# Sort loop of a graph network: the last one-hot tile in buffers of its own, and all gather products ahead of the counting

## The chip, the core and the metric

The kernel runs on one core of a Trainium2 chip. A core has five engines that run side by side, each with its own queue of instructions, and that wait for each other through semaphores: TensorE (matrix products; in the profile PE for the products and PEld for the loads of the stationary operand), VectorE (DVE), ScalarE (ACT), GpSimd (POOL) and SyncE (SP, which here only starts transfers). TensorE writes into PSUM, a small memory from which VectorE and ScalarE read; all other tiles lie in SBUF. The metric is the device time of one execution in microseconds, the median of several runs; lower is better.

## What is computed

The reference is a stack of four graph layers on 12,500 nodes with 412,500 directed edges, each between a layer norm with ReLU. The first layer is the one that matters here:

```python
h = jnp.maximum(_layernorm(x, axis=-1), 0.0)
x_j = h[dst]
m = jnp.einsum('ei,ej,ijh->eh', x_j, edge_attr_8, W_msg_tp) * norm
m = silu(m) @ W_msg_lin * norm_lin
agg = segment_sum(m, src)          # messages summed at the source nodes
```

For each edge the features of its destination node meet eight edge attributes and a weight table, pass through SiLU, and are summed at its source node. Three more layers (L1, L2 with layer norms on 64-wide edge features, L3) use the same edges again.

## The kernel before

**The sort.** The edges come ordered by destination. Before the layers, one loop (`sort_edges`, L355) brings them into a fixed layout that all layers then use. The nodes are cut into 98 windows of 128 destination nodes. Inside a window, edges are sorted into 128 cells by their source's block (`S`), 32 places a cell: that makes `TC` = 32 tiles of 128 edges. Edges beyond 32 in a cell go to `TO` = 5 more tiles, "the tiles beyond the cells". So a window has `TT` = 37 tiles. The loop runs twice over 49 windows (L400), and each pass is written out instruction by instruction with a fixed order on TensorE, VectorE, ScalarE and SyncE: these engines' order is that of the Python code, and no scheduler changes it.

**A step.** In step `g` of a pass several windows are at work, each at another age. The newest (age 0) has its records loaded: `keys` computes each edge's cell, `hot_cells` (L511) makes a one-hot tile of it, and `count` (L513 to L521) multiplies that with a triangle and with ones on TensorE, 36 products in bf16 into the PSUM bank `po`, so that each edge learns how many come before it. The window of age 1 has `look_up`, `rank` and `scatter` (L523 to L594): VectorE reads the counts out of `po` (L528 is the first instruction), works out the row of each edge, and GpSimd writes the records there with 35 indirect transfers (L588). `look_up` of a window stands at the head of the step after its count. Two and one steps before the oldest age the sorted records are read back, their slots transposed (`slot_rows`, L604) and loaded (`load_rows`).

**The first layer's messages, for the oldest window** (age 5, `old`). They are made in the same step. `hot_rows` (L615), one step ahead, turns slots into one-hot tiles on VectorE: three tiles, one for each of `PARTS`, 16, 16 and 5 edge tiles wide. `gather(i)` (L623) multiplies four of the 37 edge tiles at a time with the window's node table `win`, in f32 on TensorE, into a PSUM bank `pl`, of which there are two: gathers 0 to 3 read the first one-hot tile, 4 to 7 the second, and 8 and 9 (four tiles and one) the third. `products(i)` (L633) multiplies bank `i` with the edge attributes on VectorE and so frees the bank. `message(p)` (L648) sums and applies SiLU. `hot_sources` (L643) makes a further one-hot tile on VectorE, and `to_sources` (L661 to L666) uses it in 32 f32 products that add the messages at their sources.

**The order around the change.** In the second half of a step the code reads (L434 to L454): products 4, gather 6, products 5, gather 7; `count` of the new window; `hot_sources`, products 6, gather 8, products 7, gather 9, message 1; `hot_rows` of the next window; products 8 and 9, message 2, `to_sources`. On TensorE the count thus stands between gather 7 and gather 8. All three one-hot tiles of `hot_rows` come from one group of three buffers, so each is written where the same tile of the step before lay.

Of the kernel before, what the change touches and what calls it, by code (L numbers as in the profile page):

```python
# [11 lines left out]
F32 = mybir.dt.float32  # L12
# [7 lines left out]
P = 128  # L20
# [10 lines left out]
TC = CELLS * CAP // P  # L31
TO = 5
# [17 lines left out]
def tile_gnn(ctx: ExitStack, tc: tile.TileContext, a: dict, out: bass.AP):  # L50
# [15 lines left out]
    @contextmanager  # L66
    def banks(**bufs):

        with tc.tile_pool(name="psum", bufs=1, space=bass.MemoryType.PSUM) as pool:
            now[:] = [(pool, bufs)]  # L70
            yield
# [252 lines left out]
    def window_starts(wk):  # L324


        n = NB * TS
        di = wk.tile([P, n], I32, name="ws_di")
        sp.dma_start(di, a["dst"].rearrange("(p j) -> p j", p=P))
        v.tensor_single_scalar(di, di, 7, op=ALU.arith_shift_right)  # L330
        df = wk.tile([P, n], F32, name="ws_df")
        v.tensor_copy(df, di)
        est = wk.tile([P, P], F32, name="ws_est")
        part = wk.tile([P, P], F32, name="ws_part")
        hit = wk.tile([P, n], F32, name="ws_hit")
        at = wk.tile([P, 4], F32, name="ws_at")
        num = wk.tile([P, 4], F32, name="ws_num")
        v.memset(est, 0.0)
        for j in range(4):
            v.tensor_scalar(at[:, j:j + 1], df[:, 0:1], float(j), None, op0=ALU.add)  # L340
            v.tensor_scalar(hit, df, at[:, j:j + 1], None, op0=ALU.is_equal)
            v.tensor_reduce(num[:, j:j + 1], hit, AX.X, ALU.add)
            v.tensor_scalar(part, iota_row, at[:, j:j + 1], num[:, j:j + 1], op0=ALU.is_gt, op1=ALU.mult)
            v.tensor_add(est, est, part)
        every = wk.tile([P, P], F32, name="ws_every")
        gp.partition_all_reduce(every, est, P, bass_isa.ReduceOp.add)
        v.tensor_copy(est_i, every[0:1, :])
# [7 lines left out]
    def sort_edges():  # L355


        with tc.tile_pool(name="ws", bufs=1) as wk:
            window_starts(wk)
        with tc.tile_pool(name="so1", bufs=1) as one, tc.tile_pool(name="so", bufs=2) as ed, \  # L360
                banks(acc=4, po=1, pc=1, pl=2):
            k = {}
            k["empty"] = one.tile([P, TT, WORDS], F32, name="empty")
            v.memset(k["empty"], 0.0)
            v.memset(k["empty"][:, :, W_LS:W_LD + 1], NONE)
            k["tri"] = one.tile([P, P], BF16, name="tri")
            gp.memset(k["tri"], 1.0)
            gp.affine_select(out=k["tri"], in_=k["tri"], compare_op=ALU.is_gt, fill=0.0, base=0,
                             pattern=[[1, P]], channel_multiplier=-1)
            k["ones_bf"] = one.tile([P, P], BF16, name="ones_bf")  # L370
            v.memset(k["ones_bf"], 1.0)
            k["ones_f"] = one.tile([P, P], F32, name="ones_f")
            v.memset(k["ones_f"], 1.0)
            k["before"] = one.tile([P, TL, TL], F32, name="before")
            gp.memset(k["before"], 1.0)
            gp.affine_select(out=k["before"], in_=k["before"], compare_op=ALU.is_gt, fill=0.0, base=0,
                             pattern=[[1, TL], [-1, TL]], channel_multiplier=0)
            k["dump"] = one.tile([P, TL], F32, name="dump")
            gp.iota(k["dump"], pattern=[[P, TL]], base=ND * RM, channel_multiplier=1,
                    allow_small_or_imprecise_dtypes=True)  # L380
            v.memset(tall, 0.0)
            v.memset(cur, 0.0)

            nought = one.tile([P, 512], BF16, name="nought")
            v.memset(nought, 0.0)
            acc = [bank("acc") for _ in range(4)]
            for b in acc:
                pe.matmul(b, lhsT=nought[:, 0:P], rhs=nought, start=True, stop=True, skip_group_check=True)

            k["cells"] = dram_disjoint_views(cells, SG)  # L390
            k["slots"] = dram_disjoint_views(slot_lo, SG)

            k["parted"] = [one.tile([P, TC, 4, 16], F32, name=f"parted{b}") for b in range(2)]
            for t in k["parted"]:
                v.memset(t, 0.0)
            k["ps"] = bank("po")
            k["pc"] = bank("pc")
            v.tensor_copy(k["pc"][:, 0:P], iota_row)
            et = mybir.EngineType
            with tc.For_i(0, ND, SG) as i, tc.manual_schedule(engines={et.PE, et.DVE, et.Activation, et.SP}):  # L400
                ws = [Window(i, g, k, ed) for g in range(SG)]
                ws[0].load()
                for g in range(SG + LAG):
                    def at(lag):
                        return [ws[g - lag]] if 0 <= g - lag < SG else []
                    for w in at(-1):
                        w.load()
                    for w in at(LAG - 2):
                        w.read_back()
                    for w in at(LAG - 1):  # L410
                        w.load_rows()
                    for w in at(1):
                        w.look_up()
                        w.rank()
                        w.scatter()
                    old, new = at(LAG), at(0)
                    for w in old:
                        w.gather(0)
                        w.gather(1)
                        w.products(0)  # L420
                        w.gather(2)
                        w.products(1)
                        w.gather(3)
                    for w in new:
                        w.keys()
                    for w in old:
                        w.products(2)
                        w.gather(4)
                        w.products(3)
                        w.gather(5)  # L430
                        w.message(0)
                    for w in new:
                        w.hot_cells()
                    for w in old:  # L434
                        w.products(4)
                        w.gather(6)
                        w.products(5)
                        w.gather(7)
                    for w in new:
                        w.count()  # L440
                    for w in old:
                        w.hot_sources()
                        w.products(6)
                        w.gather(8)
                        w.products(7)
                        w.gather(9)
                        w.message(1)
                    for w in at(LAG - 1):
                        w.hot_rows()
                    for w in old:  # L450
                        w.products(8)
                        w.products(9)
                        w.message(2)
                        w.to_sources(acc)  # L454
                    for w in at(LAG - 2):
                        w.slot_rows()
                v.tensor_scalar(cur, cur, float(SG * P), None, op0=ALU.add)
            ok = one.tile([1, 1], F32, name="ok")
            v.tensor_scalar(ok, tall[0:1, 0:1], float(E), None, op0=ALU.is_equal)
            v.scalar_tensor_tensor(cells_i, tall[0:1, 1:2], float(TO * P), ok, op0=ALU.is_le, op1=ALU.mult)  # L460
            got = ed.tile([C, CELLS, 16], F32, name="wide", bufs=1)
            by_bank = got.rearrange("n (q b t) f -> b n t q f", q=4, b=4)
            for b in range(4):
                for q in range(4):
                    sc.copy(by_bank[b][:, :, q, :], acc[b][0:C, :].rearrange("n (t q f) -> n t q f", t=8, q=4)[:, :, q, :])
            with tc.If(nc.values_load(cells_i[0:1, 0:1], min_val=0, max_val=1) > 0):
                sp.dma_start(t_acc.rearrange("(s q) f -> q s f", q=C), got)

    class Window:
# [145 lines left out]
        def hot_rows(self):  # L615

            self.hots, self.got = [], {}
            for t0, k in PARTS:
                hot = self.ed.tile([P, 16 * P], F32, name="hot_dt0", bufs=3)
                v.tensor_scalar(hot[:, :k * P], self.u[:, t0 * P:(t0 + k) * P], iota_col, None, op0=ALU.is_equal)  # L620
                self.hots.append(hot)

# [1037 lines left out]
```

## Time and profile before

| | us |
|---|---|
| median of three runs | 21783.42 (21761.8 to 21790.21) |
| profiled execution | 22519.72 |
| its span, first to last instruction | 22518.0 |
| sort loop, first pass without its start and end | 470 to 3564 |
| sort loop, second pass without its start and end | 3991 to 7059 |
| mean granted TensorE clock | 0.75 |

| engine | busy us | share of the span |
|---|---|---|
| PE (products) | 15015.6 | 67% |
| PEld (loads) | 12155.3 | 54% |
| DVE | 13682.8 | 61% |
| POOL | 6955.3 | 31% |
| ACT | 3671.3 | 16% |

A row of the profile names the line of the kernel, the engine, the operation, the tiles (out<-in), the shapes and a count; after the first bar stand the busy time in all and the mean of one in ns, after the second the idle time of the engine just before such instructions and what ended most of it. "<-remote" there means that a semaphore came and that no instruction of the core was on record just before it. In a time line the columns are start, duration, engine, line, operation, and in brackets the idle time before it. Ends of TensorE's products are modelled, not seen. The profiled execution is 736 us longer than the median run without the profiler.

### The profile page before, as it was taken

How to read it: one execution, taken by the hardware profiler on the slowest of the kernel's cores; microseconds unless marked ns; L12 is line 12 of the kernel's file. 1: busy time of each engine (PE TensorE's matmuls, PEld its weight loads, DVE VectorE, ACT ScalarE, POOL GpSimd, SP SyncE). 2: the span in 40 equal slices, each digit the busy share in tenths (PEclk: the TensorE clock that was granted, in tenths of full speed). 3: DMA queues.
4: the chain of work that ended last, by engine and by line, in shares of the span. 5: the costliest groups of instructions: out<-in, count | busy, mean ns of one | idle time of the engine just before them, and what ended most of it. 6: DMA issues, size and time to landing. Idle time of an engine off the chain costs nothing. (4 is left out here: it accounts for less than half of the span.)

```text
span 22518.0 us, 475030 instructions
## 1 busy us (share of the span) xinstructions
PE 15015.6 (67%) x201276; PEld 12155.3 (54%) x201641; DVE 13682.8 (61%) x23150; ACT 3671.3 (16%) x8161; POOL 6955.3 (31%) x6387
## 2 busy tenths in 40 slices
PE   2444443444445888876666788888798988666665
PEld 1444443344444666655656566666566666544544
DVE  4666666666665666745555466666476765455455
ACT  0000000000001555510000122222222222000000
POOL 3444444444553333311111011111022221233233
PEclk7666666666666999967777699899799997566566
DMA  1000010000001222211111243344333332121121
GB/s 60 26 26 28 27 30 24 28 28 28 28 28 27 71 68 68 71 29 31 31 31 31 75 128 121 119 125 125 101 108 102 107 96 76 43 51 50 43 51 51
DMA packets 1081319, 1344.35 MB, mean 60 GB/s; under 512 B 474914, under 2 KB 629010, under 8 KB 1078374
## 3 DMA queue, kind: packets, MB, share of 16 engines
q1 hardware_dynamic: 799088, 1232.52, 17.4%
q0 software_dynamic: 258720, 76.68, 3.4%
q8 instruction: 1638, 26.84, 0.5%
q10 hardware_dynamic: 21462, 4.95, 0.1%
q14 instruction: 411, 3.37, 0.0%
HBM read 954.24 MB, written 359.21 MB: 58 GB/s over the span
## 5 line engine op out<-in xcount | busy, mean ns | idle before, releaser
L588 POOL DMA_INDIRECT cells<-rec,s_row x3430 | 3418.3, 997 | 3488.0 <-DVE s_row L584 2237.1
L630 PE MATMUL pl<-win,hot_dt 128*128 128x128 f32 x7252 | 1461.5, 371 | 2038.2 <-DVE wide L639 1533.3
L1350 POOL DMA_INDIRECT xo<-t_src,c x980 | 1139.8, 1163 | 5279.7 <-ACT lod L1095 1912.4
L630 PEld LDWEIGHTS pl<-win,hot_dt 128*128 128x128 f32 x7252 | 1341.0, 278 | 2143.9 <-DVE wide L639 1569.3
L1005 PE MATMUL po<-tab,hot_s 98*32 98x16 f32 x75264 | 1458.2, 204 | 1215.2 <-issue 725.5
L997 DVE TENSOR_TENSOR hot_d<-iota_row,c 128x1024 f32<-128x1024 f32 (+1 forms) x1470 | 1649.4, 1141 | 867.0 <-PE pa L1046 499.7
L664 PE MATMUL acc<-parted,hot_s 128*98 128x64 f32 x6272 | 1219.2, 352 | 1296.8 <-issue 1287.5
L1005 PEld LDWEIGHTS po<-tab,hot_s 98*32 98x32 f32 x75264 | 1240.8, 138 | 1473.6 <-issue 1154.2
L1119 DVE TENSOR_REDUCE nsum<-sq 128x8 f32<-128x512 f32 (+1 forms) x1470 | 946.6, 644 | 1588.9 <-ACT sq L1116 1422.9
L1010 POOL DMA_INDIRECT xw<-t_gc,c x980 | 1102.8, 1125 | 2545.3 <-DMA c<-cells 980.9
L664 PEld LDWEIGHTS acc<-parted,hot_s 128*98 128x98 f32 x6272 | 1117.9, 269 | 1419.3 <-issue 1409.8
L1164 PE MATMUL pa<-hot,y 128*64 128x128 f32 x21756 | 1686.0, 286 | 174.7 <-issue 92.7
L1133 DVE TENSOR_TENSOR hot<-iota_row,lod 128x512 f32<-128x512 f32 x2352 | 1513.7, 685 | 1.5 <-remote 1.1
L1046 PE MATMUL pa<-prod,hot_d 128*128 128x130 f32 x7252 | 1227.5, 336 | 416.4 <-DVE prod L1040 373.5
L1164 PEld LDWEIGHTS pa<-hot,y 128*64 128x64 f32 x21756 | 1244.0, 140 | 452.9 <-issue 192.9
L620 DVE TENSOR_SCALAR hot_dt<-u,iota_col 128x2048 f32<-128x2048 uint8 (+1 forms) x294 | 296.2, 1038 | 1961.2 <-remote 1883.2
L1116 ACT ACTIVATE sq<-po 128x512 f32<-128x512 f32 (+1 forms) x1470 | 831.0, 565 | 3668.4 <-PE po L1113 2995.0
L1046 PEld LDWEIGHTS pa<-prod,hot_d 128*128 128x128 f32 x7252 | 1129.1, 243 | 456.7 <-issue 434.8
L770 POOL DMA_INDIRECT g_l<-summed,row x490 | 810.2, 1653 | 1675.3 <-ACT summed L766 1447.7
L1386 PE MATMUL po<-ft,eb_w0e 128*64 128x512 f32 (+1 forms) x3920 | 1030.5, 594 | 296.8 <-DMA ft<-e_feat 276.9
L1010 POOL DMA_INDIRECT xo<-t_h,c x490 | 478.5, 976 | 2317.4 <-DMA c<-cells 1249.4
L1453 PE MATMUL pa<-hot_d,xw 128*32 128x128 f32 x14504 | 897.7, 374 | 369.3 <-DVE xw L1445 164.6
(363 smaller groups left out, 27049.8 us busy)
## 6 DMA issues: line engine op xcount, KB each, us to landing
e_feat<-ft SPq DMA_DIRECT2D x882, 256.0 KB
ft<-e_feat SPq DMA_DIRECT2D x882, 256.0 KB
c<-cells SPq DMA_DIRECT2D x392, 296.0 KB
places<-slot_lo SPq DMA_DIRECT2D x294, 392.0 KB
ud<-slot_lo SPq DMA_DIRECT2D x98, 1024.0 KB
c<-cells SPq DMA_DIRECT2D x147, 592.0 KB
us<-slot_lo SPq DMA_DIRECT2D x98, 784.0 KB
u<-slot_lo SPq DMA_DIRECT2D x98, 592.0 KB
```

What stands on the lines that cost most here:

```text
L588: ins = gp.indirect_dma_start(out=self.cells, out_offset=bass.IndirectOffsetOnAxis(ap=self.row[:, t:t + 1], axis=0), in_=self.rec[:, t, :] ...
L630: pe.matmul(pl[:, t * P:(t + 1) * P], lhsT=self.hots[t0 // 16][:, o:o + P], rhs=self.win, start=True, stop=True, skip_group_check=True)
L664: pe.matmul(acc[t // 8][0:C, o:o + 64], lhsT=self.hot[:, t, :], rhs=self.k["parted"][self.g % 2][:, t, :, :].rearrange("p q f -> p (q f)") ...
L997: v.tensor_tensor(o[:, :k, :], bc_mid(iota_row, k), bc_last(c[:, t0:t0 + k, W_LD], P), ALU.is_equal)
L1005: pe.matmul(out[CAP * q:CAP * (q + 1), t * w:(t + 1) * w], lhsT=oht[:, o:o + CAP], rhs=tab[:, TC * q + t0 + t, :], start=start, stop=True, ...
L1010: gp.indirect_dma_start(out=out[:, t, :], out_offset=None, in_=table, in_offset=bass.IndirectOffsetOnAxis(ap=c[:, TC + t, W_SRC:W_SRC + 1] ...
L1046: pe.matmul(acc[:, 0:130], lhsT=hot[:, t, :], rhs=prod[:, t, :], start=t0 + t == 0, stop=t0 + t == TT - 1)
L1119: return lambda: v.tensor_reduce(self.sums[:, 8 * c:8 * c + 2 * k], sq[:, :2 * k, :], AX.X, ALU.add)
L1133: v.tensor_tensor(hot[:, w].rearrange("p (h t) d -> p h t d", h=2), iota_row[:, None, None, :].to_broadcast([P, 2, 2, P]), lo[:, :, :, Non ...
L1164: pe.matmul(self.acc[64 * w:64 * w + 64, 0:P], lhsT=lhsT, rhs=rhs, start=c == 0 and i < 2, stop=c == 9 and i >= len(work) - 2, skip_group_ ...
L1350: gp.indirect_dma_start(out=self.xo[:, w, t, :], out_offset=None, in_=t_src[s], in_offset=bass.IndirectOffsetOnAxis(ap=self.c[:, w, TC + t ...
L1386: pe.matmul(out[64 * h:64 * h + 64], lhsT=lhsT, rhs=rhs, start=start, stop=stop, skip_group_check=True)
```

## The change

Two edits, both in the sort loop:

1. In `hot_rows`, the third one-hot tile of a step (the one for the tiles beyond the cells) is taken from a group of its own, `hot_do0`, with two buffers of 5 x 128 elements. The first two stay in the group of three buffers.
2. In the step, products 6, gather 8, products 7, gather 9 and message 1 of the old window now come ahead of the new window's `count`; `hot_sources` comes after them, just ahead of `hot_rows`.

```diff
                         w.products(5)
                         w.gather(7)
-                    for w in new:
-                        w.count()
-                    for w in old:
-                        w.hot_sources()
                         w.products(6)
                         w.gather(8)
                         w.products(7)
                         w.gather(9)
                         w.message(1)
+                    for w in new:
+                        w.count()
+                    for w in old:
+                        w.hot_sources()
                     for w in at(LAG - 1):
                         w.hot_rows()
...
             for t0, k in PARTS:
-                hot = self.ed.tile([P, 16 * P], F32, name="hot_dt0", bufs=3)
+                if t0 < TC:
+                    hot = self.ed.tile([P, 16 * P], F32, name="hot_dt0", bufs=3)
+                else:
+                    hot = self.ed.tile([P, TO * P], F32, name="hot_do0", bufs=2)
                 v.tensor_scalar(hot[:, :k * P], self.u[:, t0 * P:(t0 + k) * P], iota_col, None, op0=ALU.is_equal)
                 self.hots.append(hot)
```

From the changed place on, lines of the kernel stand three lower than before (L620 becomes L623, L630 L633, L639 L642, L664 L667).

## The prediction

> **What bounds the loop now.** I read the costliest groups first. One VectorE row is idle far longer than busy: the third one-hot tile of a step, 1961.2 us of idle "<-remote".
>
> ```profile
> L630 PE MATMUL pl<-win,hot_dt 128*128 128x128 f32 x7252 | 1461.5, 371 | 2038.2 <-DVE wide L639 1533.3
> L620 DVE TENSOR_SCALAR hot_dt<-u,iota_col 128x2048 f32<-128x2048 uint8 (+1 forms) x294 | 296.2, 1038 | 1961.2 <-remote 1883.2
> ```
>
> Then the busy time by stretch, for the two passes of the sort loop without their starts and ends (columns: stretch, its length, then busy us of PE, PEld, DVE, ACT and POOL):
>
> ```profile
> 470.00:3564.00 3094.00, 1440.56 (x7702) 1296.28 (x7701) 1975.82 (x3166) 174.28 (x439) 1535.22 (x1539) 0.61 0.09 27
> 3991.00:7059.00 3068.00, 1429.71 (x7703) 1291.37 (x7703) 1976.28 (x3168) 174.47 (x440) 1536.22 (x1539) 0.61 0.09 27
> ```
>
> These 88 full steps take 6162 us, 70.0 each. VectorE works 45 us of a step and POOL 35, so no engine is full; VectorE waits 22.3 us of every step in one place. The time line of VectorE in one step (start, duration) shows where:
>
> ```profile
> 3053.72 1.28 DVE L639 TENSOR_TENSOR wide<-pl,c 128x512 f32<-128x512 f32 x2
> 3054.92 3.42 DVE L645 TENSOR_TENSOR hot_s<-pc,c 128x3136 f32<-128x3136 f32 x1
> 3058.25 1.28 DVE L639 TENSOR_TENSOR wide<-pl,c 128x512 f32<-128x512 f32 x2
> 3059.63 2.29 DVE L651 TENSOR_REDUCE pre<-wide 128x256 f32<-128x2048 f32 x1
> 3061.84 2.47 DVE L620 TENSOR_SCALAR hot_dt<-u,iota_col 128x2048 f32<-128x2048 uint8 x2
> 3083.67 0.55 DVE L620 TENSOR_SCALAR hot_dt<-u,iota_col 128x640 f32<-128x640 uint8 x1 [19.36 <-remote]
> 3084.14 0.88 DVE L639 TENSOR_TENSOR wide<-pl,c 128x512 f32<-128x512 f32 x2
> 3085.12 0.82 DVE L651 TENSOR_REDUCE pre<-wide 128x80 f32<-128x640 f32 x1
> 3085.86 0.28 DVE L528 COPY s_num<-po 128x128 f32<-128x128 f32 x1
> ```
>
> The third hot_dt takes over the buffer that the old window's gather 9 reads, so it waits for gather 9. TensorE in the same step:
>
> ```profile
> 3057.76 2.08 PE L520 MATMUL po<-s_ohs,tri 128*128 128x256 bf16 x18
> 3059.67 2.02 PE L520 MATMUL po<-s_ohs,ones_bf 128*128 128x256 bf16 x17
> ...
> 3064.43 2.14 PE L630 MATMUL pl<-win,hot_dt 128*128 128x128 f32 x8 [1.15 <-issue]
> 3066.58 1.08 PE L664 MATMUL acc<-parted,hot_s 128*98 128x64 f32 x5
> ```
>
> Gather 9 looks done at 3066.6, yet VectorE is let go at 3083.67. The semaphore updates in the trace settle it: gather 8's came at 3080.84 and gather 9's at 3083.65, 15 and 17 us after their records; gathers 6 and 7 had theirs 14 ns and 0.1 us after. So TensorE truly ends late here. Between the record of gather 9 and its update about 62 further weight loads and matmuls were issued: [...] at the end one entry per 0.70 us. It is slow while POOL issues the 35 row scatters of the step (35 x (0.96 + 0.30) = 44.2 us, from 22.4 to 66.6 us after the step's first look-up instruction, L528), and the backlog of L664 runs off at 12 a us from 71 us on. Over the 88 steps gather 9 lets go between 60 and 72 us: 49 steps last 66.9 us on average, 39 last 73.9.
>
> [...]
>
> **Part by part.** The order of instructions is the same on ACT, POOL and SP; no DMA is added, dropped or moved past another. I put L528 of a step at 0.
>
> *Own buffers for the third tile.* It no longer waits for gather 9: 0.55 us of work leaves the far side of the wait, and the price is 2 x 640 x 4 B of SBUF a partition and no time. The two large tiles keep three buffers for two a step, so they wait for nothing new.
>
> *Gathers 8 and 9 ahead of the count.* On TensorE they are 5 matmuls, issued as 20 loads and passes; the count is 36 loads and 36 matmuls. The sum, 92, and their start (after gather 7, 38.5 us) stay. Gathers 8 and 9 now end near 40 us if the queue moves, 42 to 58 if it does not; VectorE needs them only at 48. Of the last steps of a pass, the first has no count but a scatter; there the third tile waited 1.02 us, not 22: gathers 8 and 9 do get through when nothing stands before them.
>
> *The wait moves to L528.* It reads the count's result. Before, waiting for gather 9 covered it; now it waits itself, for the end of the count, which is now the last of the same 92 entries. Behind it in VectorE's queue stands the whole look-up, and behind that POOL's next scatters. The start of the loop shows this wait bare, when no window is old enough to gather:
>
> ```profile
> 297.70 2.95 PE L520 MATMUL po<-s_ohs,ones_bf 128*128 128x256 bf16 x18
> ...
> 349.24 0.29 DVE L528 COPY s_num<-po 128x128 f32<-128x128 f32 x1 [55.29 <-remote]
> ```
>
> The count alone was held 49 us while scatters ran. So I take it that the 92nd entry ends when it did, 60 to 72 us. What VectorE did between the release and L528 (0.55 + 0.88 + 0.82 with overlap: 3085.86 - 3083.67 = 2.19 us) is then already done. Gain: 88 x 2.19 = 193 us.
>
> *hot_sources later.* It stood between products 5 and 6 and covered 3.4 us while TensorE made gathers 6 and 7. Now products 6 waits for gather 6 (37.2 us, VectorE free at 35.6: 1.6 us) and products 7 for gather 7 (38.6: 0.7 us). VectorE then runs products 7 to 39.3, the sum 41.6, hot_sources 45.1, three one-hot tiles 48.0, products 8 and 9, the sum, and is at L528 at about 49.8 us. That is below 60, so it is hidden in full steps by the wait for the count. In the ten last steps (five a pass), which have no count, up to 2 us each is bare: 20 us lost.
>
> Sum against the profiled execution (span 22518.0, 22519.7 with its ends): -193 + 20 = -173 us. The runs without the profiler have a median of 21783, 736 less; I put the same change there: **21,610 us** (-0.8%).
>
> Does the stall exist without the profiler? All but the 88 steps is 22518 - 6162 = 16356 us of span. If that costs no more without profiling, 21783 leaves 5427 us, 61.7 a step: still 14 us above what VectorE needs. So most of the wait is real.
>
> **Rivals.**
>
> *A, the wait moves (55%).* As above. For it: equal order sum, the wait at 349. Own range 21,540 to 21,720.
>
> *B, the count gets out early (14%).* If the slow entries are the f32 ones, 0.70 us each at the end (2.81 us for gather 9's four), the bf16 count would end sooner now that they are ahead. [...] Then the 49 shorter steps would last some 57.4 us instead of 66.9 and the 39 long ones lose A's 2.2: 49 x 9.5 + 39 x 2.2 = 551 us, less the 20 of the last steps, gives 21,250. Against it: in long steps the count crawls too, and at 264 to 349 it was held with no f32 matmul near.
>
> *C, slower: no stall without the profiler (13%).* [...] If so, TensorE ends the 92 at about 45.6 to 46.3 us and L528 stood at 47.8 to 48.5 before; after, VectorE's 49.8 binds, because hot_sources lost its cover. 88 x 1.65 + 20 = +165: 21,950. It decides once the 92 entries end before 47.6 us. Against it: the 61.7 us above.
>
> *D, more long steps (18%).* The shorter step leaves TensorE 2.2 us less rest between scatters, and short steps now are often followed by long ones (correlation of neighbours -0.19). If the 39 long ones become all 88, each at 72.0: 88 x (72.0 - 70.0) = +172, 21,955. Long steps would be 71.8 and short ones 64.7, so the gain is gone when 73% are long instead of 44%. I spread D from 21,700 to 21,955.
>
> **How the numbers follow.** The forecast is A's. The range leaves out the better half of B and the upper ends of C and D: 21,290 to 21,960. 0.2% is 44 us, about what the spread of the three runs (28 us) allows to be told: faster is below 21,740: A nearly whole (0.53), B (0.14) and a little of D (0.02): 0.69; within: a third of D, the slow edge of A, 0.09; slower: C and half of D, 0.22.
>
> **What would show it.** In the profile after: the third one-hot tile's idle time near 0; L528 idle by about 18 us in 88 steps, its releaser the count; products 6 and 7 with small waits on gathers; steps of 64 to 72 us, about 68 on average. Wrong if L528 starts at 55 us or earlier (B), if steps are longer than 70 (D), or if the profiled span falls and the runs without profiling rise (C).

## The result, and the profile after

| | us |
|---|---|
| before, median of 4 runs | 21,772.6 (21,745 to 21,790) |
| after, median of 4 runs | 22,000.3 (21,945 to 22,033) |
| ratio, 95% interval | 1.0103 (1.0079 to 1.0127) |
| traced execution of after, its span | 21,995.6 |

The change made the kernel 1.0% slower, +228 us. Forecast was 21,610 us; the time also lies 40 us above the range. The traced execution of after took 21,997.4 us and is one of the four runs; the traced execution of before (22,518 us of span, "the first trace" below) is not among the runs of before. Against that trace after looks 522 us faster; against the timed runs it is 228 us slower.

The two passes of the loop after, by stretch (columns as for before; the last three are the granted TensorE clock, the busy share of the DMA engines and GB/s):

```profile
470.00:3295.00 2825.00, 1367.17 (x7667) 1207.86 (x7668) 1961.48 (x3111) 173.20 (x439) 1522.09 (x1528) 0.63 0.10 29
3705.00:6600.00 2895.00, 1374.06 (x7765) 1221.05 (x7762) 2000.04 (x3181) 175.20 (x442) 1555.72 (x1566) 0.63 0.10 29
```

VectorE still does its 45 us a step. The groups of the loop on VectorE (after the first bar busy time and mean ns, after the second the idle time before and its releasers) show where it now waits:

```profile
L642 DVE TENSOR_TENSOR wide<-pl,c 128x512 f32<-128x512 f32 x980 | 611.5, 646 | 1256.6 <-remote 828.5 <-PE pl L633 348.5 <-issue 79.1
...
L623 DVE TENSOR_SCALAR hot_do<-u,iota_col 128x640 f32<-128x640 uint8 x98 | 53.5, 546 | 0.0
L528 DVE COPY s_num<-po 128x128 f32<-128x128 f32 x98 | 28.4, 290 | 646.7 <-remote 529.8 <-PE po L520 105.5 <-issue 11.1
```

The third one-hot tile (`hot_do`) never waits: edit 1 does what it says. The wait went to the reader of the count (L528, 647 us) and, more of it, to the products (L642, 1257 us). From one start of L528 to the next, the 88 full steps of after last 65.28 us on average, but none lasts that: 37 last 49.5 to 57.8 us and 51 last 70.2 us or more. I call the short ones free and the long ones held. One of each kind on VectorE, the step that ends at 1240.77 and the one that ends at 1315.01:

```profile
1225.02 1.28 DVE L642 TENSOR_TENSOR wide<-pl,c 128x512 f32<-128x512 f32 x2
1227.86 0.69 DVE L642 TENSOR_TENSOR wide<-pl,c 128x512 f32<-128x512 f32 x1 [1.57 <-PE pl L633]
1229.30 0.69 DVE L642 TENSOR_TENSOR wide<-pl,c 128x512 f32<-128x512 f32 x1 [0.74 <-PE pl L633]
...
1240.77 0.29 DVE L528 COPY s_num<-po 128x128 f32<-128x128 f32 x1 [0.49 <-remote]
...
1285.91 0.69 DVE L642 TENSOR_TENSOR wide<-pl,c 128x512 f32<-128x512 f32 x1 [6.34 <-remote]
1304.10 0.69 DVE L642 TENSOR_TENSOR wide<-pl,c 128x512 f32<-128x512 f32 x1 [17.50 <-remote]
...
1315.01 0.28 DVE L528 COPY s_num<-po 128x128 f32<-128x128 f32 x1
```

In the free step TensorE keeps up and VectorE waits only 1.57 and 0.74 us, for gathers 6 and 7, which nothing covers any more (cover is work that VectorE does while TensorE makes what it needs next). Over the 37 free steps these two waits are 1.57 and 0.93 us on average; in 34 of them the reader of the count waits afterwards too, 3.23 us on average over the 37. In the held step the gathers themselves are stuck. TensorE in that step:

```profile
1286.66 2.07 PE L633 MATMUL pl<-win,hot_do 128*128 128x128 f32 x8 [4.95 <-DVE wide L642]
1304.85 0.80 PE L633 MATMUL pl<-win,hot_do 128*128 128x128 f32 x2 [16.12 <-DVE wide L642]
1305.44 3.94 PE L520 MATMUL po<-s_ohs,tri 128*128 128x256 bf16 x18
```

Gather 9, the last two entries of the first kind, comes 16 us after gather 8: it needs the bank that products 7 frees, and products 7 had to wait 17.50 us for gather 7. That is near the end of POOL's row scatters (the last one ends at 1307.2), and the count stands behind it. So one trace holds two regimes, and the experiments had to tell what the change costs in each.

### The profile page after: what moved, and what is told of

Its sections match the earlier page's. It is cut to its first block, busy times and chain, and to the rows that moved or that the text cites. A ratio compares the mean times of both kernels' runs of the same rounds, so it can differ in the third digit from the quotient of the medians.

```text
span 21995.6 us, 475491 instructions
## 1 busy us (share of the span) xinstructions
PE 14866.9 (68%) x201641; PEld 11976.8 (54%) x201641; DVE 13696.7 (62%) x23150; ACT 3670.5 (17%) x8161; POOL 6932.1 (32%) x6387
## 5 line engine op out<-in xcount | busy, mean ns | idle before, releaser
L633 PE MATMUL pl<-win,hot_dt 128*128 128x128 f32 x6272 | 1169.8, 365 | 1380.0 <-DVE wide L642 1044.6
L633 PEld LDWEIGHTS pl<-win,hot_dt 128*128 128x128 f32 x6272 | 1112.4, 275 | 1434.9 <-DVE wide L642 1076.8
L667 PE MATMUL acc<-parted,hot_s 128*98 128x64 f32 x6272 | 1104.1, 337 | 839.1 <-issue 741.5
L667 PEld LDWEIGHTS acc<-parted,hot_s 128*98 128x98 f32 x6272 | 1014.5, 254 | 935.4 <-issue 927.0
L642 DVE TENSOR_TENSOR wide<-pl,c 128x512 f32<-128x512 f32 x980 | 611.5, 646 | 1256.6 <-remote 828.5
L994 DVE TENSOR_SCALAR hot_s<-places,iota_col 98x1024 f32<-98x1024 uint8 x1176 | 848.7, 749 | 422.5 <-remote 356.1
```

The costliest lines, as they stand in the source:

```text
L633: pe.matmul(pl[:, t * P:(t + 1) * P], lhsT=self.hots[t0 // 16][:, o:o + P], rhs=self.win, start=True, stop=True, skip_group_check=True)
L667: pe.matmul(acc[t // 8][0:C, o:o + 64], lhsT=self.hot[:, t, :], rhs=self.k["parted"][self.g % 2][:, t, :, :].rearrange("p q f -> p (q f)") ...
```

## Experiments

T1 is rival C: VectorE's chain sets the step, and the loss is the cover that `hot_sources` gave to gathers 6 and 7. T2 is the forecast's view: TensorE is held beside the scatters in all conditions. The runs went to several chips, which proved to differ: each comparison is with runs of before on the same chip. On three of them before takes 18,644 to 18,660 us ("free chips"); on a fourth 22,630 us ("the held chip"). The differences in us are between medians; the recorded ratios are not ratios of these medians, and the two can disagree by up to 17 us, on the held chip by up to 36. Wherever before was traced, that execution takes about as long as the other runs of its chip: 18,671 us with a median of 18,644, 18,661 with 18,660, and 22,546 with a range of 22,519 to 22,683.

### Is there a stall at all? (free chip)

**The loop of before run twice**: the same loop in `for again in range(2)`, with this ahead of the second run.

```diff
+                if again:
+                    v.memset(tall, 0.0)
+                    v.memset(cur, 0.0)
+                    for b in acc:
+                        pe.matmul(b, lhsT=nought[:, 0:P], rhs=nought, start=True, stop=True, skip_group_check=True)
```

> The kernel before with its whole sort loop run twice (the second time from the same start, so the output is the same). The time less that of before is the loop's own time without the profiler. T1 (the stall of TensorE beside the row scatters belongs to the profiler; without it VectorE's chain of about 48 us sets the step): 88 x 48 + some 800 us of starts and ends = about 5,000 us. T2 (the stall is there without the profiler too; the 736 us are a part of it that the profiler adds): 7,021 us of loop in the profile less 736 = about 6,280 us.

Measured: 23,427.1 against 18,652.6 us, so the loop takes 4,775 us. T2's 6,280 is out here.

**The loop of after run twice**, the same edit in the kernel after.

> The kernel after with its sort loop run twice. T1 and T2 both expect the loss of 228 us to lie in the loop: the second loop costs about 228 us more than that of the kernel before (T1: about 5,200 us; T2: about 6,500 us, near the 6,544 us of its profile). If it costs no more, the loss lies outside the loop.

Measured: 23,966.3 us, 539 more than the loop of before twice, 270 a loop. The loss lies in the loop.

**The loop of before twice, the first one without scatters.**

```diff
-                            w.scatter()
+                            if again:
+                                w.scatter()
```

> The kernel before with its loop twice, the first of the two without the 35 row scatters of each window (its records aren't placed; the second loop does it properly). Against the loop twice with scatters in both. T1: without the profiler nothing is held by the scatters, VectorE's chain sets the step either way: within 100 us of it. T2: TensorE is no longer held beside POOL's scatters, the step falls from some 61 us to VectorE's 48: at least 1,050 us less.

Measured: 23,363.2 us, 64 less than with scatters in both: full steps of 46.82 us without them and 47.34 with them. On this chip the scatters cost half a microsecond a step.

**A second one-hot of the sources where VectorE waits in the first trace.**

```diff
                         w.message(1)
+                        w.hot_sources()
                     for w in at(LAG - 1):
                         w.hot_rows()
```

> The kernel before with a second, unused one-hot comparison of the sources (3.42 us of VectorE) in each step, just ahead of the three one-hot tiles, which is where VectorE waits in the profile. T1: VectorE has no wait there without the profiler, so all of it shows: 98 x 3.42 = +335 us, at least +235. T2: it falls into the wait for gather 9: within 50 us of the kernel before.

Measured: +368 us (1.0192, 1.0175 to 1.0209): no wait there to hide it. Full steps last 50.58 us, 3.23 more than in before, which makes 284 us; most of the rest lies at the ends of the passes, since the second, later tile is the one that `to_sources` reads (see the next section).

### Both kernels, traced side by side (free chip)

**Before and after, unchanged.**

> The kernel before, unchanged, for its trace on the same chip as the runs beside it. T1 (here VectorE's chain sets the step): steps of about 47.3 us, as in the loop run twice, no idle time at the third one-hot tile, and the time within 0.3% of the runs of before. T2 (TensorE held): steps near 62 us or more with the third one-hot tile idle for some 15 us.

> The kernel after, unchanged, beside before on one chip. T1: steps of 50.0 instead of 47.3 us, because products 6 and 7 (and later ones) wait for their gathers: 88 x 2.7 + some 25 us in the ten last steps = +265 us, all of it as waits of the products. T2: TensorE is held, steps alternate between 50 and 75 us, and the difference is in the wait of the count's reader (L528).

Measured: after 18,925.1 against 18,643.7 us, +281 (1.0160, 1.0143 to 1.0177). VectorE in one step of before:

```profile
1069.84 1.28 DVE L639 TENSOR_TENSOR wide<-pl,c 128x512 f32<-128x512 f32 x2
1071.03 3.41 DVE L645 TENSOR_TENSOR hot_s<-pc,c 128x3136 f32<-128x3136 f32 x1
1074.36 1.28 DVE L639 TENSOR_TENSOR wide<-pl,c 128x512 f32<-128x512 f32 x2
...
1077.94 2.94 DVE L620 TENSOR_SCALAR hot_dt<-u,iota_col 128x2048 f32<-128x2048 uint8 x3
...
1082.52 0.28 DVE L528 COPY s_num<-po 128x128 f32<-128x128 f32 x1
```

And of after:

```profile
1058.39 1.28 DVE L642 TENSOR_TENSOR wide<-pl,c 128x512 f32<-128x512 f32 x2
1061.24 0.69 DVE L642 TENSOR_TENSOR wide<-pl,c 128x512 f32<-128x512 f32 x1 [1.57 <-PE pl L633]
1062.94 0.69 DVE L642 TENSOR_TENSOR wide<-pl,c 128x512 f32<-128x512 f32 x1 [1.01 <-PE pl L633]
1064.10 2.29 DVE L654 TENSOR_REDUCE pre<-wide 128x256 f32<-128x2048 f32 x1 [0.46 <-DVE wide L642]
1066.30 3.42 DVE L648 TENSOR_TENSOR hot_s<-pc,c 128x3136 f32<-128x3136 f32 x1
```

Before, the third one-hot tile follows the others without a gap: the wait that edit 1 removes does not exist here. After, products 6, products 7 and the sum behind them stand bare for 1.57 + 1.01 + 0.46 us, while `hot_s` comes too late to cover them; over the 88 steps the two products wait 1.57 and 0.97 us on average, and not at all in before. Full steps go from 47.35 to 49.96 us: 88 x 2.61 = 230. The join of the two passes, where old windows run out with no count, goes from 156.6 to 184.7 us, and the loop has two such ends: 56. Sum 286; measured 281.

Most of these 56 us have another cause than the lost cover. The sums of `to_sources` need `hot_s`, and the gathers of the next window stand behind them on TensorE. Here are the sums of one window in an ending step of before, and VectorE's first wait in the step after it:

```profile
2493.01 6.33 PE L664 MATMUL acc<-parted,hot_s 128*98 128x64 f32 x64
2500.49 0.69 DVE L639 TENSOR_TENSOR wide<-pl,c 128x512 f32<-128x512 f32 x1 [2.18 <-PE pl L630]
```

And of after:

```profile
2610.62 10.90 PE L667 MATMUL acc<-parted,hot_s 128*98 128x64 f32 x64 [5.32 <-DVE hot_s L648]
2623.69 0.69 DVE L642 TENSOR_TENSOR wide<-pl,c 128x512 f32<-128x512 f32 x1 [8.64 <-PE pl L633]
```

TensorE waits 5.32 us for the late `hot_s`, and then the same 64 passes take 10.90 us at a granted clock of 0.50, against 6.33 at 0.89. In a full step the look-up keeps VectorE busy meanwhile; in an ending step nothing does, and products 0 wait for gather 0: for the last four windows of a pass this wait is 8.2 to 8.7 us in after and 1.2 to 6.4 in before, together 22.5 of the 28 us of one end. The waits of the loop in before (total us, times, longest):

```profile
DVE wide L639 <- PE pl L630: 57.6, 100, 6.4
```

and in after:

```profile
DVE wide L642 <- PE pl L633: 287.2, 273, 8.6
```

### Which part costs it? (free chips)

**The cover put back**, all else as after.

```diff
                         w.gather(7)
+                        w.hot_sources()
                         w.products(6)
...
                         w.count()
-                    for w in old:
-                        w.hot_sources()
```

> The kernel after with the one-hot comparison of the sources put back between gather 7 and products 6; the buffers of their own and the gathers ahead of the count stay. T1: VectorE's cover is back, the waits of the products fall by some 260 us: within 60 us of before. T2: the loss comes from the count's place behind the gathers, and stays: within 60 us of after.

Measured: 18,635.6 us, 1.0002 (0.9993 to 1.0011) of before; on another free chip 0.9994 (0.9984 to 1.0004). The whole loss is gone; on a free chip the count's new place and the buffers together neither cost nor bring anything.

**The buffers alone.**

> The kernel before with only the one-hot buffers of their own. T1: the third one-hot tile waits for nothing any more or never did; within 30 us of before where VectorE sets the step. T2: where gather 9 holds it, the wait moves to the count's reader (L528) and 2.2 us of each step come out of it: about -190 us.

Measured: 1.0005 (0.9997 to 1.0014). Nothing, as T1 has it.

**The cover taken away alone**: before, with one line moved.

```diff
-                        w.hot_sources()
                         w.products(6)
...
                         w.message(1)
+                        w.hot_sources()
```

> The kernel before with only the comparison of the sources moved, from between gather 7 and products 6 to just after the second message; the count, the gathers and the buffers stay. T1 (where VectorE sets the step, the whole loss is the 3.4 us of work that lay over gathers 6 and 7): all of the loss, +280 us within 40, with waits of about 1.6 and 1.0 us ahead of products 6 and 7. Rival T3 (the loss needs the count's new place as well): within 60 us of before.

Measured: +276 us (1.0146, 1.0129 to 1.0162), full steps of 49.96 us and a join of 184.7, as in after. One moved line is the whole loss here, at the ends too.

**Another cover**: after, with the three one-hot tiles of the next window in that place.

```diff
                         w.gather(7)
+                    for w in at(LAG - 1):
+                        w.hot_rows()
+                    for w in old:
                         w.products(6)
...
                         w.hot_sources()
-                    for w in at(LAG - 1):
-                        w.hot_rows()
-                    for w in old:
                         w.products(8)
```

> The kernel after with the three one-hot tiles of the next window (2.9 us of VectorE) moved up to between gather 7 and products 6, where the comparison of the sources stood; that comparison stays late. T1: any VectorE work in that place covers gathers 6 and 7, so the waits of the products fall again and the time is within 60 us of before. Rival T4 (it is the late one-hot of the sources itself, which the sums into acc (L664 before, L667 here) wait for): the time stays within 60 us of after, +280.

Measured: +74 us (1.0033, 1.0021 to 1.0046), 14 outside T1's 60, but its trace says why: full steps last 47.37 us, as in before, and the join of the passes lasts 193.1 instead of 156.6; 2 x 36.5 = 73. An ending step of this kernel:

```profile
2494.22 3.41 DVE L648 TENSOR_TENSOR hot_s<-pc,c 128x3136 f32<-128x3136 f32 x1
2497.78 10.89 PE L667 MATMUL acc<-parted,hot_s 128*98 128x64 f32 x64 [3.91 <-DVE hot_s L648]
2510.85 0.69 DVE L642 TENSOR_TENSOR wide<-pl,c 128x512 f32<-128x512 f32 x1 [11.49 <-PE pl L633]
```

So in full steps it is any work in that place, and T4 falls; at the ends of the passes T4 is right: `hot_s` comes even later than in after, the sums wait for it, and with them the next window's gathers.

### What else binds VectorE's step? (free chip)

**The one-hot tiles made on ACT**, in the kernel before.

```diff
-                v.tensor_scalar(hot[:, :k * P], self.u[:, t0 * P:(t0 + k) * P], iota_col, None, op0=ALU.is_equal)
+                sc.activation(hot[:, :k * P], self.u[:, t0 * P:(t0 + k) * P], AF.Square, bias=iota_neg)
+                sc.activation(hot[:, :k * P], hot[:, :k * P], AF.Relu, bias=one_col, scale=-1.0)
```

> The kernel before with the three one-hot tiles of a window made on ACT, idle for most of the loop, as the square of u less the row number and then the positive part of 1 less that, instead of one comparison on VectorE. T1: VectorE's step of 47.3 us loses the 2.9 us of the three tiles and nothing else binds before POOL's 35 row scatters (35 x 1.26 = 44.2 us): 44.4 us a step, 98 x 2.9 = -285 us at most, at least -200. T2 (VectorE has slack, TensorE is held): within 40 us of before.

Measured: -86 us (0.9951, 0.9935 to 0.9968): faster than before and after, but a third of what T1 said. The tiles were themselves a cover: in this kernel products 8 and 9 follow message 1 at once and wait for gathers 8 and 9, which stand behind the count; the products' waits rise from 58 to 226 us. Full steps fall to 46.07 us, not 44.4.

**The same with the cover put back and the gathers ahead of the count.**

> The version with own buffers, gathers ahead of the count and the cover put back, with the three one-hot tiles made on ACT. T1: as the kernel before with these tiles on ACT, and better than it where products 8 and 9 would otherwise wait for gathers 8 and 9 behind the count (4.1 us on TensorE): between 0 and -60 us against that one. If POOL's scatters bind at 44.2 us a step, the two are equal.

Measured: +30 us (1.0014, 1.0003 to 1.0024), 116 us above the version that it should have equalled or beaten. Its waits (L531 is the reader of the count here):

```profile
DVE s_num L531 <- PE po L523: 277.6, 97, 7.0
DVE wide L646 <- PE pl L637: 95.0, 105, 10.6
```

Now the reader of the count waits in every step, 278 us instead of 56: the count stands behind all gathers on TensorE, and VectorE gets there sooner. That is the forecast's "the wait moves to L528", on a chip where TensorE is never held.

### Where TensorE is held

**Before, after and the cover put back**, on the held chip.

> The kernel before, unchanged, to get its trace in the condition of the verdict (before at 21,773 us). If TensorE is held there: third one-hot tile idle in many steps, steps of 60 us and more. If not (before at 18,645 us again): steps of 47.3 us.

> The kernel after, unchanged, beside it. T1 (lost cover): +228 to +280 us over before in either condition, with waits of 1.6 and 1.0 us at products 6 and 7. T2 (longer hold): the loss shows as waits of products and of the count's reader for gathers and a count that are held.

> The kernel after with the one-hot of the sources put back over gathers 6 and 7. T1: the loss is gone in either condition (within 60 us of before). T2: where TensorE is held the loss stays, within 60 us of after.

Measured: before 22,629.6 us; after 1.0037 (1.0026 to 1.0049), about +84 by the ratio and +76 by the medians; the cover put back 1.0029 (1.0012 to 1.0045), about +65 and +30. For after, T1's +228 to +280 is out here. The intervals of the last two overlap, and the latter is inside T1's 60 by the medians and outside by the ratio: the times tell nothing of what the cover is worth here.

The waits on VectorE in before:

```profile
DVE hot_dt L620 <- remote: 1790.4, 83, 26.8
```

and in after:

```profile
DVE s_num L528 <- remote: 1476.9, 77, 54.9
DVE wide L642 <- remote: 413.4, 116, 6.3
```

| full steps (88) | under 60 us | 60 to 70 | 70 to 73 | 73 and more | mean |
|---|---|---|---|---|---|
| first trace of before | 0 | 46 | 3 | 39 | 70.04 |
| before, held chip | 3 | 32 | 14 | 39 | 70.15 |
| after, held chip | 0 | 0 | 88 | 0 | 71.68 |
| cover put back, held chip | 7 | 6 | 68 | 7 | 70.33 |

The first trace of before looks like the held chip's, by its steps and by its time (22,519.7 us; 22,519 to 22,683 there). In every step of after, L528 follows the end of the last scatter: that end comes 67.5 us (median) after the L528 before, and the next L528 4.3 us later. In the long steps of before it is 67.6 and 6.4 us. So the two edits together do save the 2.2 us of the forecast in those (74.2 to 71.9). But before also had steps of 62 to 70 us, in which gather 9 and with it the count got out about when the scatters ended or while the last few still ran; after has none: the count, now behind all gathers, comes only once the scatters are over. With the cover put back the count stands in the same late place, and 75 of 88 steps last 70 us or more as well, which points to the count's place and not to the late `hot_s`. Each row is one execution.

**The loop twice on this chip, the first time without scatters** (the same edit as on the free chip; the first loop's records aren't placed).

> The kernel before with its loop run twice, the first of the two without the row scatters (its records aren't placed, the second loop does it properly). If the scatters are what holds TensorE: the first loop takes some 47 us a step, about 4,700 us, while the second takes 1,000 us or more longer. If TensorE isn't held, or by something else: both take the same within 100 us.

Measured: one stretch of a pass without scatters and one with them:

```profile
2900.00:4800.00 1900.00, 928.67 (x7184) 885.30 (x7184) 1811.67 (x2906) 161.84 (x410) 0.00 (x0) 0.73 0.11 35
5150.00:8600.00 3450.00, 1552.04 (x8541) 1400.87 (x8541) 2145.32 (x3416) 195.56 (x491) 1662.18 (x1671) 0.62 0.09 27
```

Without scatters all full steps last 46.8 us, as on a free chip; with them 70.7. The scatters hold TensorE on this chip (88 x 23.9 = 2,103 us a loop), and on the free chip where this was tried they do not (half a microsecond a step). The granted clock does not explain it: from 297 to 349 us, where the first counts stand alone on TensorE, it is 0.53 in the first trace and in the held chip's, and 0.60 on a free chip, while the reader of the count waits up to 55.2 us on the one and at most 7.0 us on the other.

**Before and the cover put back once more**, to find the condition of the timed runs (21,773 us).

> The kernel before, unchanged, for a trace in the condition of the verdict (before at 21,773 us). Mixed: steps fall in two groups, near 47.3 us where the count and gather 9 get out before the scatters end, near 66 to 74 us where they don't, with a mean of about 61.7 us over full steps; the first group is larger than or as large as that of after (37 of 86).

> The kernel after with the one-hot of the sources put back over gathers 6 and 7. In the condition of the verdict: if the loss is the lost cover of the free steps, within 80 us of before; if it is the count's place at the end of the queue, +150 us or more. Where nothing is held: within 60 us of before. Where nearly all is held: +30 us within 60.

Measured: a free chip again, with full steps of 47.35 us (before 18,660 us; the cover put back, 0.9994, is told above). The mixed steps that were expected of before did not show.

## Why the prediction was wrong

**What bounds the loop now.** Right for the trace it was read from, wrong for the runs it was to predict. The reading itself (TensorE held beside the row scatters, gather 9 let go late) stands: without scatters the held chip's steps fall from 70.7 to 46.8 us.

**The step that failed: "Does the stall exist without the profiler?"** and its answer, "61.7 a step: still 14 us above what VectorE needs. So most of the wait is real". Two errors lie in it. The 736 us between the first trace and the runs were taken for the profiler's, but on every chip here a traced execution takes about as long as the other runs. What differs is the condition of the executions, and moving the forecast by the same 736 us carried the condition of one over to the other. And 61.7 is a mean: the trace of after shows steps of 50 and of 72 us, none near its mean of 65.28. A mean above VectorE's 48 was taken for a wait in every step, where a part of the steps may have had none at all. On the free chips, where no step has one, the cover counted in every step.

**"hot_sources later ... hidden in full steps by the wait for the count".** This is where the time went on the free chips. The sizes were right: products 6 and 7 waits of 1.6 and 0.7 us foreseen, 1.57 and 1.01 measured; VectorE's chain 47.8 to 48.5 before and 49.8 after foreseen, 47.35 and 49.96 measured. The cover that was to hide them was the stall. The ten last steps cost 56 us there, not 20, and by a path that the forecast left out: `to_sources` gets its one-hot tile later, and the next window's gathers wait behind it. The cover put back removes both.

**Rival C (13%)** had the mechanism and the place of the loss for the free condition: +165 us foreseen, +281 measured, since the step before was a little shorter and the ends dearer. "It decides once the 92 entries end before 47.6 us" fits: they do on a free chip, where the count's 72 entries take 4.1 us (1074.15 to 1078.27 us in the trace of before). That the stall was the profiler's, which C also said, is wrong.

**The forecast A (55%)** was right in its mechanism where TensorE is held (-2.2 us in the long steps, idle time at L528 in every step of after on the held chip), but "the 92nd entry ends when it did" held for long steps only. **Rival D (18%)** is what the held chip shows: "the 39 long ones become all 88, each at 72.0", +172 us; measured 88 of 88 at 71.2 to 72.1, +84 by the runs, +175 between the two traces. That its number fits so well is in part luck: its reason, less rest for TensorE between scatters, is not shown, and the traces point to the count's place instead. Its correlation of neighbouring steps, -0.19, comes out as -0.32 from the 88 steps of the first trace. **Rival B**'s sign, L528 at 55 us or earlier, is seen in most of the 37 free steps of after (32 of them); but its 57.4 us for the shorter steps was the author's estimate, which no trace or run shows. B would have made the kernel faster, and the free chips show why such a step is no gain: there before has it as well, and shorter.

**What stays open.** No trace of before exists from the condition of the timed runs (21,773 us). The trace of after there is a mix, 37 free steps and 51 held ones. An estimate from the free chips: 37 x 2.61 + 56 = 153 of the 228 us come from the late `hot_sources`, and the rest are held steps and waits for the count. How many steps of before were free there isn't known, and in 34 of the 37 free steps it is the count that VectorE waits for last; so this split is argued and not shown. That the late `hot_sources` is the whole loss is shown for the free chips alone. What makes one chip hold TensorE beside scatters and three others not is open too; the held chip was seen in one session only, and the mixed trace shows both kinds of step in one execution, so that it is the chip itself isn't shown either. Which of the two edits saves the 2.2 us of the long steps was not tried on the held chip.

## What to carry to other kernels

Before an instruction is moved for a wait that a trace shows, ask what it covers now and what on another engine waits for its result, and price the move once with that wait gone: here one moved line cost +276 us where the stall was absent. Where a trace and the timed runs differ by several per cent, they may show different conditions, as they did here; a mean step carried from one to the other may describe no step at all, so look at the steps one by one and forecast each kind.

## What the runs showed of the hardware

The same program takes 18,650 or 22,630 us on two chips of one type. The VectorE and GpSimd instructions compared last the same on both (a row scatter 0.96 us with 0.30 after it, `hot_s` 3.41 and 3.42 us); on the one, TensorE crawls while GpSimd issues row scatters (27 matrix products from 5044 to 5064 us of that chip's trace of before, and in the first trace 33 from 3066 to 3083 us beside 14 scatters), and on the other it does not (149 from 1058 to 1084 us of the trace of before, beside 20 scatters). The loop makes up about 2,230 us of the 3,870 us between a trace of before on a free chip and the one on the held chip. Behind it GpSimd issues 490 other indirect transfers (L770), and there the two run level: from the first to the last it is 2,307 us on the free chip and 2,304 us on the held one. The rest of the difference lies in later stages and was not looked into.

The first trace's 55 us of waiting for a bare count at the start of the loop is at most 7 us on the free chips. On a free chip, the 64 passes of a window's sums take 10.90 us after a wait of 5.32 us, at a granted clock of 0.50, and 6.33 us without the wait, at 0.89. ACT makes a 128x2048 one-hot in two passes of 2.00 us each, against one of about 1.28 us on VectorE.
